# Layer 0 of a four-layer kernel: the preparation of each chunk spread over 24 slots, a column-ordered projection read contiguously and written permuted, and Z's copy placed ahead of the exponential

## The chip, the cores and the metric

The kernel runs on one core of one Trainium2 chip. The metric is the device time of one execution in microseconds, as the median of three runs. Engines are called as in the profile: PE is the matrix engine, PEld its weight loads, DVE the vector engine, ACT the scalar engine, POOL the general engine, SP the engine that issues DMA transfers here. A "q" behind a name (SPq) is the engine's sequencer.

## The reference

The model has four layers; only layer 0 is touched. After a group norm, an input projection and a depthwise convolution, it runs a selective scan in four directions (row order, column order, and both reversed) over 4096 positions, for 256 channels with 16 states each, for two batch elements:

```
dts, Bs, Cs = split(einsum('bkdl,kcd->bkcl', xs, x_proj_w))
dts   = einsum('bkrl,kdr->bkdl', dts, dt_proj_w)
delta = softplus(dts + dt_bias)
for each position:
    h = exp(delta * A) * h + (delta * u) * B
    y = sum over states of h * C
```

The four results are added in image order, normalised, gated and projected.

## The kernel before

**Tiling.** Each batch element is one pass of the same code. Its work is 32 chunks: four directions, in the order 0, 2, 1, 3, by eight chunks of 512 positions. Directions 1 and 3 read the image in column order. A chunk has two halves of 256 positions, and a half has eight slots; a slot holds four groups of 128 channel-state pairs by 256 positions. The list `todo` holds the chunks, `NS` is 512 slots, and the loop `for s in range(NS)` (from L471) is one slot per pass. `where(s)` turns a slot into chunk, direction, half and place `j` in the half. In this text slots of a chunk are counted 0 to 15, and the first half is 0 to 7.

**One slot.** All order is written by hand (`tc.manual_schedule`): each engine runs its instructions in the order in which the Python code issues them. A slot issues, in this order:

- `make_inputs(s + 2)` in even slots: on POOL, L391 multiplies a 1 MB tile `row` (delta times u, one row for eight channels, repeated over the states by the load) by `bt` (B) into the state tile `S`, for two slots. L396 and L397 add the carried state. `S` has two buffers, each for one half of a chunk.
- `decays(s + 2)`: four PE products at L411 give delta times A in one of three PSUM tiles `dA`.
- `exponent(s + 1)`: ACT takes exp of `dA` at L425.
- the scan on DVE at L482, in place in `S`.
- one step of `contract` (L432 on), a generator that sums the states of the previous half. Its products (L443) write one PSUM tile `Z`, four times per half; ACT copies `Z` to `ze` (L449), and SP stores it (L453). It has seven steps, in places 0 to 6 of a half, and products in steps 0 to 5. The tile `W` (C, from L430) is loaded in places 2 to 5, for use in the next half.
- one step of each open `prologue`, the generator that prepares a chunk.
- `load_rows(s + 7)` in odd slots: the next `row` (L379), with three buffers.

**The preparation.** `prologue(i + 2)` starts in slot 1 of chunk i and takes one step per slot, so parts of two prologues are open at a time. It projects u (L296, the product named px; `in_order` gives u in the order of the direction), copies the result to `xd` (L299, L301), stores B and C to DRAM (`bcd`, L303 and L304), forms delta's argument (L311), computes softplus in pieces on ACT (L313 to L322) and POOL (L323, L325), sums the pieces on PE by a product with the identity (L333), copies delta to `dt` (L336), multiplies by u on DVE (L337), stores that to DRAM as `drow` (L339), and at the end gets `bt` (L346), `dg` (L344) and the factor `ea` for the carried state (L353, L354). The tiles `r`, `e`, `u`, `l` and `xd` have one buffer each. PSUM is full: three `dA` tiles of two banks, one bank for `Z` and one (tag `ps`) for all products of the prologue.

**SP.** Nearly all transfers of the layer are issued by SP in program order on one queue. The build gives them eight completion semaphores in turn, so a transfer is issued only once the one eight before it has landed.

Of the kernel before, what the change touches and what calls it, by code (L numbers as in the profile page):

```python
# [16 lines left out]
F32 = mybir.dt.float32  # L17
# [3 lines left out]
ALU = mybir.AluOpType  # L21
# [142 lines left out]
def layer0(k, x, x0):  # L164
# [14 lines left out]
    with ExitStack() as es:  # L179
# [21 lines left out]
        def in_order(h, kk, c):  # L201
            if kk % 2:
                u = U[:, h, :].rearrange("p (g i w j) -> p w g j i", g=4, i=16, w=4)[:, c // 2]
            else:
                u = U[:, h, (c // 2) * 1024 : (c // 2 + 1) * 1024].rearrange("p (i w j) -> p w i j", i=16, w=4)
            return u[:, 2 * (c % 2) : 2 * (c % 2) + 2]

        for b in range(B):
# [60 lines left out]
            with ExitStack() as e2:  # L269
# [19 lines left out]
                def prologue(i):  # L289


                    kk, c = todo[i]
                    m = 64 * (kk % 2)
                    px = ps.tile([P, CH], F32, name="pd", tag="ps")
                    for h in range(2):
                        nc.tensor.matmul(px[m : m + 64], w_xp[:, h, kk, :], in_order(h, kk, c), start=h == 0, stop=h == 1)  # L296
                    yield
                    xd = one.tile([P, CH], F32, name="xd")
                    nc.scalar.copy(xd[m : m + 32], px[m : m + 32])  # L299

                    nc.scalar.copy(xd[m + 32 : m + 64].rearrange("p (e t a r) -> p e t a r", e=4, t=4, a=8), px[m + 32 : m + 64].rearrange("p (e a t r) -> p e t a r", e=4, a=8, t=4))  # L301
                    bcd = ddr.tile([32, CH], F32, name="bcd")
                    nc.sync.dma_start(out=bcd[:16], in_=xd[m + 8 : m + 24, :])  # L303
                    nc.sync.dma_start(out=bcd[16:], in_=xd[m + 32 : m + 48, :])  # L304
                    yield
                    yield
                    r, e, u, l = (one.tile([P, 2, CH], F32, name=n) for n in ("r", "e", "u", "l"))
                    for h in range(2):
                        bias = k.v("dt_b")[:, kk * 2 + h : kk * 2 + h + 1]
                        pd = ps.tile([P, CH], F32, name="pd", tag="ps")  # L310
                        nc.tensor.matmul(pd, w_dt[m : m + 8, kk // 2, h * P : (h + 1) * P], xd[m : m + 8, :], start=True, stop=True)  # L311
                        yield
                        nc.scalar.activation(e[:, h, :], pd, AF.Abs, bias=bias)  # L313
                        nc.scalar.activation(r[:, h, :], pd, AF.Relu, bias=bias)
                        yield
                    nc.scalar.activation(e, e, AF.Exp, scale=-1.0)
                    yield
                    nc.scalar.activation(u, e, AF.Identity, bias=1.0)
                    yield
                    nc.scalar.activation(l, u, AF.Ln)  # L320
                    yield
                    nc.scalar.activation(u, u, AF.Identity, bias=-1.0)  # L322
                    nc.gpsimd.tensor_tensor(r, r, l, ALU.add)  # L323
                    yield
                    nc.gpsimd.tensor_tensor(e, e, u, ALU.subtract)  # L325
                    yield
                    yield
                    dt = two.tile([P, 2, CH], F32, name="dt")
                    drow = ddr.tile([2, 8, 8, 2, 2, T], F32, name="drow")
                    for h in range(2):  # L330
                        pd = ps.tile([P, CH], F32, name="pd", tag="ps")
                        for n, t in enumerate((r, e)):
                            nc.tensor.matmul(pd, k.ident, t[:, h, :], start=n == 0, stop=n == 1)  # L333
                        yield
                        v = lambda t: t.rearrange("p (a b c) -> p a b c", a=2, b=16)
                        nc.scalar.copy(dt[:, h, :], pd)  # L336
                        nc.vector.tensor_tensor(v(r[:, h, :]), v(pd), in_order(h, kk, c), ALU.mult)  # L337
                        for a in range(2):
                            nc.sync.dma_start(out=drow[:, :, :, a, h].rearrange("s d g t -> (d g) s t"), in_=r[64 * a : 64 * a + 64, h, :].rearrange("p (s t) -> p s t", s=2))  # L339
                        if h == 0:  # L340
                            yield
                    f = T - 1 if kk >= 2 else 0
                    dg = one.tile([P, 2, 16, 2], F32, name="dg")
                    nc.gpsimd.tensor_tensor(dg, pick.unsqueeze(1).unsqueeze(3).to_broadcast([P, 2, 16, 2]), dt[:, :, f::T].rearrange("p h s -> p s h").unsqueeze(2).to_broadcast([P, 2, 16, 2]), ALU.mult)  # L344
                    bt = two.tile([P, CH], F32, name="bt")
                    nc.sync.dma_start(out=bt, in_=bass.AP(bcd.tensor, bcd.offset, [[CH, 16], [0, 8], [1, CH]]))  # L346
                    for _ in range(7):
                        yield
                    pe = ps.tile([P, CH], F32, name="pd", tag="ps")
                    nc.tensor.matmul(pe[:, :64], own, dg.rearrange("p s g h -> p (s g h)"), start=True, stop=True)  # L350
                    yield
                    ea = two.tile([P, 2, 32], F32, name="ea")
                    nc.vector.tensor_tensor(ea, pe[:, :64].rearrange("p (s g) -> p s g", s=2), an2[:, kk * 32 : kk * 32 + 32].unsqueeze(1).to_broadcast([P, 2, 32]), ALU.mult)  # L353
                    nc.scalar.activation(ea, ea, AF.Exp)  # L354
                    ready[i] = dt, drow, bcd, bt, ea


                NS = 16 * len(todo)
# [73 lines left out]
                def contract(n):  # L432

                    i, kk, sub, _ = where(8 * n)
                    S, W = Ss[n], Ws[n % 2]
                    t0 = (todo[i][1] * CH + sub * T) // P
                    for f in range(4):
                        Z = pz_.tile([P, 4, 32, 4], F32, name="Z")
                        for a in range(4):
                            for q in range(4):  # L440
                                w = W[:, f // 2].rearrange("p d t -> p (d t)")[:, 16 * (f % 2) + 4 * a + q :: 32]
                                t = 64 * f + 16 * a + q
                                nc.tensor.matmul(Z[32 * q : 32 * q + 32, :, :, a].rearrange("p t g -> p g t"), w, S[:, :, t : t + 13 : 4], start=True, stop=True)  # L443
                            if a == 1 and f in (0, 3):
                                yield
                        yield
                        if f % 2 == 0:
                            ze = two.tile([P, 4, 32, 8], F32, name="ze")
                        nc.scalar.copy(ze[:, :, :, 4 * (f % 2) : 4 * (f % 2) + 4], Z)  # L449
                        if f % 2:  # L450
                            for t in range(4):
                                dst = ydr[b][kk, t0 + f // 2, 4 * t : 4 * t + 4].rearrange("q d g a -> (q d) (g a)")
                                nc.sync.dma_start(out=dst, in_=ze[t::4, t].rearrange("p g a -> p (g a)"))  # L453

                with tc.manual_schedule():
# [10 lines left out]
                    decays(1)  # L466
                    exponent(0)
                    soon, back = [prologue(1)], None
                    for _ in range(15):
                        next(soon[0])  # L470
                    for s in range(NS):  # L471
                        i, kk, sub, j = where(s)
                        S, dA = Ss[s // 8], dAs[s % 3]
                        if j % 2 == 0:
                            make_inputs(s + 2)
                        if s % 16 == 1 and i + 2 < len(todo):
                            soon.append(prologue(i + 2))
                        decays(s + 2)
                        exponent(s + 1)
                        s_ = slice(None, None, -1) if kk >= 2 else slice(None)  # L480
                        flat, dflat = (t.rearrange("p g t -> p (g t)")[:, s_] for t in (S[:, 4 * j : 4 * j + 4, :], dA))
                        nc.vector.tensor_tensor_scan(flat, dflat, flat, 0.0, ALU.mult, ALU.add)  # L482
                        if j == 0 and s > 0:
                            back = contract(s // 8 - 1)
                        if back is not None:
                            if next(back, back) is back:
                                back = None
                                del Ss[s // 8 - 1]
                        if j in (2, 3, 4, 5):
                            for d in (2 * j - 4, 2 * j - 3):  # L490
                                load_c(s // 8, d)
# [1274 lines left out]
```

## Time and profile before

| What | us |
|---|---|
| Median of three runs | 15351.72 |
| Lowest and highest | 15348.02, 15357.47 |
| The profiled execution's own time | 15384.23 |
| Its span | 15382.4 |
| First scan to last scan of the first batch element | 177.7 to 1815.5 |
| First scan to last scan of the second | 2198.4 to 3843.7 |

The profile page and all times inside it are of one execution, whose span is 15382.4 us; some 3283 us of it (1637.8 + 1645.3) are the two loops that the change touches. Within a row of groups, the first numbers behind the bar are busy time and mean ns of one instruction, then idle time of the engine just before, with the instruction that ended it. Matmul ends are modelled and overlap, so the time of a stream of products is read from start to start. A product in f32 stands as two records.

### The profile page before, as it was taken

How to read it: one execution, taken by the hardware profiler on the slowest of the kernel's cores; microseconds unless marked ns; L12 is line 12 of the kernel's file. 1: busy time of each engine (PE TensorE's matmuls, PEld its weight loads, DVE VectorE, ACT ScalarE, POOL GpSimd, SP SyncE). 2: the span in 40 equal slices, each digit the busy share in tenths (PEclk: the TensorE clock that was granted, in tenths of full speed). 3: DMA queues.
4: the chain of work that ended last, by engine and by line, in shares of the span. 5: the costliest groups of instructions: out<-in, count | busy, mean ns of one | idle time of the engine just before them, and what ended most of it. 6: DMA issues, size and time to landing. Idle time of an engine off the chain costs nothing.

```text
span 15382.4 us, 234681 instructions
## 1 busy us (share of the span) xinstructions
PE 12387.6 (81%) x91214; PEld 7926.4 (52%) x91214; DVE 12707.2 (83%) x11405; ACT 9497.0 (62%) x14103; POOL 13019.5 (85%) x4168
## 2 busy tenths in 40 slices
PE   7888788888777545497896888978888899898897
PEld 4544454444577413254563555645445555555565
DVE  6777657777453799999999999999999999999973
ACT  4666436655001477777777677777777777777752
POOL 5888638888287899999999999999999999999960
PEclk8999899999888767698997999989999999999998
DMA  6888748888565445465555555555666666666543
GB/s 158 200 194 196 187 105 197 197 195 191 166 199 162 148 151 167 155 203 180 194 193 171 185 189 193 199 185 191 200 190 201 191 196 204 191 196 200 189 161 134
DMA packets 1444903, 2809.37 MB, mean 183 GB/s; under 512 B 393136, under 2 KB 1110608, under 8 KB 1240784
## 3 DMA queue, kind: packets, MB, share of 16 engines
q1 hardware_dynamic: 1395936, 2638.55, 58.3%
q0 software_dynamic: 46560, 153.18, 3.3%
q8 instruction: 721, 11.81, 0.3%
q14 instruction: 390, 3.19, 0.1%
q10 hardware_dynamic: 1296, 2.63, 0.0%
HBM read 2372.53 MB, written 421.31 MB: 182 GB/s over the span
## 4 chain that ended last, share of the span: by engine, by line
POOL 43%; PE 23%; DVE 12%; DMA 10%; issue 4%; ACT 3%; SPq 3%; another core or an unknown queue 1%; POOLq 0%; ACTq 0%; DVEq 0%
POOL S L1318 36%; DVE S L1376 9%; PE pef L1202 6%; DMA row<-drow 6%; POOL S L391 3%; PE Z L443 3%; PE Z L1336 2%; POOL G L742 2%; PE dA L411 2%; DMA W<-bcd 2%; PE acc L1175 2%; SPq L430 1%; DVE S L482 1%; PE pv L756 1%; PE pd L333 1%
## 5 line engine op out<-in xcount | busy, mean ns | idle before, releaser
L1376 DVE TENSOR_TENSOR_SCAN S<-dA,S 128x512 f32<-128x512 f32 x8192 | 9225.7, 1199 | 387.5 <-ACT dA L1374 204.1
L1318 POOL TENSOR_TENSOR S<-row,g 128x4096 f32<-128x4096 f32 x1024 | 9104.3, 8898 | 241.4 <-DMA row<-drow 159.7
L1374 ACT ACTIVATE dA<-row,a_t 128x512 f32<-128x512 f32 x8192 | 5614.6, 692 | 2165.9 <-DVE S L1376 2131.1
L1336 PE MATMUL Z<-S,cv 128*32 128x256 f32 x32768 | 2506.4, 436 | 1508.1 <-ACT ze L1342 1230.9
L1202 PE MATMUL pef<-hk,ur 128*128 128x256 f32 x14336 | 3514.1, 388 | 134.7 <-ACT e L1182 116.7
L1202 PEld LDWEIGHTS pef<-hk,ur 128*128 128x128 f32 x14336 | 2646.9, 191 | 1074.4 <-issue 564.1
L482 DVE TENSOR_TENSOR_SCAN S<-dA,S 128x1024 f32<-128x1024 f32 x1024 | 2309.3, 2283 | 758.6 <-ACT dA L425 422.8
L391 POOL TENSOR_TENSOR S<-row,bt 128x2048 f32<-128x2048 f32 x512 | 2383.8, 4656 | 432.8 <-PE Z L443 334.3
L1336 PEld LDWEIGHTS Z<-S,cv 128*32 128x32 f32 x32768 | 1003.4, 121 | 2718.1 <-issue 1229.5
L443 PE MATMUL Z<-S,W 128*32 128x128 f32 x16384 | 1191.5, 434 | 438.4 <-DMA W<-bcd 218.1
L1342 ACT COPY ze<-Z 128x512 f32<-128x512 f32 x1024 | 1122.4, 1096 | 232.5 <-PE Z L1336 196.2
L425 ACT ACTIVATE dA<-dA 128x1020 f32<-128x1020 f32 x1024 | 1028.6, 1010 | 378.0 <-PE dA L411 339.3
L411 PE MATMUL dA<-dt,quad 64*128 64x255 f32 x8192 | 1183.4, 414 | 19.8 <-DVE S L482 19.3
L443 PEld LDWEIGHTS Z<-S,W 128*32 128x32 f32 x16384 | 715.0, 170 | 818.3 <-issue 288.1
L1175 PE MATMUL acc<-e,mw 128*128 128x512 f32 x1920 | 1048.4, 634 | 29.6 <-ACT e L1182 28.8
L411 PEld LDWEIGHTS dA<-dt,quad 64*128 64x128 f32 x8192 | 750.9, 195 | 580.4 <-issue 385.3
L1202 PEld LDWEIGHTS pef<-hd,ur 128*128 128x128 f32 x4096 | 758.3, 194 | 493.7 <-issue 235.0
L742 POOL DMA_INDIRECT G<-table,idx x576 | 807.2, 1401 | 219.8 <-issue 167.9
L1202 PE MATMUL pef<-hd,ur 128*128 128x256 f32 (+1 forms) x4096 | 876.7, 340 | 102.0 <-ACT e L1182 95.5
L749 DVE TENSOR_TENSOR G<-G,wt 128x4608 f32<-128x4608 f32 x64 | 317.8, 4966 | 557.0 <-DMA G<-table,idx 537.2
L1182 ACT COPY e<-pef 128x512 f32<-128x512 f32 x960 | 557.9, 587 | 109.6 <-PE pef L1202 60.7
L756 PE MATMUL pv<-ident,G 128*128 128x128 f32 x4608 | 569.2, 285 | 30.0 <-issue 29.6
(341 smaller groups left out, 7858.9 us busy)
## 6 DMA issues: line engine op xcount, KB each, us to landing
row<-drow SPq DMA_DIRECT2D x1536, 1024.0 KB
zd<-ze SPq DMA_DIRECT2D x1024, 256.0 KB
hk<-in_phi_dram SPq DMA_DIRECT2D x128, 576.5 KB
hk<-in_phi_dram SPq DMA_DIRECT2D x96, 704.5 KB
hd<-in_phi_dram SPq DMA_DIRECT2D x512, 128.5 KB
mw<-wdr SPq DMA_DIRECT2D x480, 128.0 KB
hk<-in_phi_dram SPq DMA_DIRECT2D x160, 320.5 KB
hk<-in_phi_dram SPq DMA_DIRECT2D x96, 448.5 KB
```

What stands on the lines that cost most here:

```text
L391: nc.gpsimd.tensor_tensor(S[:, o, :], rows.pop(s), bt[:, sub * T : (sub + 1) * T].unsqueeze(1).to_broadcast([P, 8, T]), ALU.mult)
L411: nc.tensor.matmul(dA[:, 2 * a + h, rest], stats[d, j][r, h, :], dt[r, h, at : at + T - 1], start=True, stop=True)
L443: nc.tensor.matmul(Z[32 * q : 32 * q + 32, :, :, a].rearrange("p t g -> p g t"), w, S[:, :, t : t + 13 : 4], start=True, stop=True)
L482: nc.vector.tensor_tensor_scan(flat, dflat, flat, 0.0, ALU.mult, ALU.add)
L742: nc.gpsimd.indirect_dma_start(out=G[:, o, :], out_offset=None, in_=table[b], in_offset=bass.IndirectOffsetOnAxis(ap=idxs[b][:, i * 9 + o ...
L1175: nc.tensor.matmul(acc.rearrange("p a s -> p (a s)"), ms[f][:, o, :], e, start=box["first"], stop="whole" in box and (f, o) == todo[-1])
L1202: nc.tensor.matmul(pe[:, a, 256 - n :], ur[:, par, j, :], h[:, at : at + n], start=i == 0, stop=i + 1 == len(mm))
L1318: nc.gpsimd.tensor_tensor(S, row.unsqueeze(1).to_broadcast([P, 2, R, T]), g.unsqueeze(2).to_broadcast([P, 2, R, T]), ALU.mult)
L1336: nc.tensor.matmul(Z[32 * j : 32 * j + 32, q], cv[:, h, s], S[:, h, :, s], start=h == 0, stop=h == 1)
L1342: nc.scalar.copy(ze.rearrange("p q t e -> p q e t"), Z)
L1374: nc.scalar.activation(dA, row[:, j % R, :], AF.Exp, scale=a_t[:, h, d : d + 1])
L1376: nc.vector.tensor_tensor_scan(s, dA, s, 0.0, ALU.mult, ALU.add)
```

## The change

The prologue starts in slot 5 instead of 1, is stepped ahead of the older one (`insert(0, ...)`), and its steps are spread out. For chunk i + 2, counted from slot 0 of chunk i (16 is slot 0 of chunk i + 1):

| Step | slot before | slot after |
|---|---|---|
| px, the projection of u | 1 | 5 |
| copies to xd, stores of bcd | 2 | 6 |
| delta's argument, halves of the channels | 4 and 6 | 8 and 10 |
| Abs and Relu | 5 and 7 | 9 and 11 |
| exp, +1, Ln | 8, 9, 10 | 12, 13, 14 |
| -1 (ACT) and r + l (POOL) | 11 | 15 |
| e - u (POOL) | 12 | 17 |
| sum of the pieces on PE | 14 and 16 | 22, both |
| copy to dt, product with u, four drow stores | 15 and 17 | 23, all |
| dg and the load of bt | 17 | 24 |
| product for ea; ea | 24; 25 | 28; 29 |

The second sum of the pieces now has a PSUM tile of its own, `pd1`, in `Z`'s bank. The order of the row loads does not change: the first `row` of chunk i + 2 is issued in slot 25 in both. Before the loop, 11 instead of 15 steps of the second chunk's prologue are run.

In directions 1 and 3 px reads u with contiguous runs of 16 and writes PSUM with a step of 16 elements (64 bytes); before, it read with a step of 64 elements and wrote contiguously.

The step of `contract`, with the copy of `Z`, is issued between the decays and the exponential of a slot; before, after the scan.

```diff
-                    m = 64 * (kk % 2)
+                    m, box = 64 * (kk % 2), [None] * 5
+                    ready[i] = box
...
                     for h in range(2):
-                        nc.tensor.matmul(px[m : m + 64], w_xp[:, h, kk, :], in_order(h, kk, c), start=h == 0, stop=h == 1)
+                        to, u = px[m : m + 64].rearrange("p (a b c) -> p a b c", a=2, b=16), in_order(h, kk, c)
+                        if kk % 2:
+                            to, u = (t.rearrange("p a b c -> p a c b") for t in (to, u))
+                        nc.tensor.matmul(to, w_xp[:, h, kk, :], u, start=h == 0, stop=h == 1)
...
                     nc.gpsimd.tensor_tensor(r, r, l, ALU.add)
                     yield
+                    yield
                     nc.gpsimd.tensor_tensor(e, e, u, ALU.subtract)
-                    yield
+                    for _ in range(5):
+                        yield
+                    pds = [ps.tile([P, CH], F32, name="pd", tag="ps"), pz_.tile([P, CH], F32, name="pd1", tag="Z")]
+                    for h in range(2):
+                        for n, t in enumerate((r, e)):
+                            nc.tensor.matmul(pds[h], k.ident, t[:, h, :], start=n == 0, stop=n == 1)
                     yield
...
                     for h in range(2):
-                        pd = ps.tile([P, CH], F32, name="pd", tag="ps")
-                        for n, t in enumerate((r, e)):
-                            nc.tensor.matmul(pd, k.ident, t[:, h, :], start=n == 0, stop=n == 1)
-                        yield
-                        v = lambda t: t.rearrange("p (a b c) -> p a b c", a=2, b=16)
-                        nc.scalar.copy(dt[:, h, :], pd)
-                        nc.vector.tensor_tensor(v(r[:, h, :]), v(pd), in_order(h, kk, c), ALU.mult)
+                        nc.scalar.copy(dt[:, h, :], pds[h])
+                    for h in range(2):
+                        nc.vector.tensor_tensor(v(r[:, h, :]), v(pds[h]), in_order(h, kk, c), ALU.mult)
                         for a in range(2):
                             nc.sync.dma_start(out=drow[:, :, :, a, h].rearrange("s d g t -> (d g) s t"), in_=r[64 * a : 64 * a + 64, h, :].rearrange("p (s t) -> p s t", s=2))
-                        if h == 0:
-                            yield
+                    box[:3] = dt, drow, bcd
+                    yield
...
-                    for _ in range(7):
+                    box[3] = bt
+                    for _ in range(4):
                         yield
...
-                    ready[i] = dt, drow, bcd, bt, ea
+                    box[4] = ea
...
-                        Z = pz_.tile([P, 4, 32, 4], F32, name="Z")
+                        Z = pz_.tile([P, 4, 32, 4], F32, name="Z", tag="Z")
...
-                    for _ in range(15):
+                    for _ in range(11):
                         next(soon[0])
...
-                        if s % 16 == 1 and i + 2 < len(todo):
-                            soon.append(prologue(i + 2))
+                        if s % 16 == 5 and i + 2 < len(todo):
+                            soon.insert(0, prologue(i + 2))
                         decays(s + 2)
-                        exponent(s + 1)
-                        s_ = slice(None, None, -1) if kk >= 2 else slice(None)
-                        flat, dflat = (t.rearrange("p g t -> p (g t)")[:, s_] for t in (S[:, 4 * j : 4 * j + 4, :], dA))
-                        nc.vector.tensor_tensor_scan(flat, dflat, flat, 0.0, ALU.mult, ALU.add)
                         if j == 0 and s > 0:
                             back = contract(s // 8 - 1)
                         if back is not None:
                             if next(back, back) is back:
                                 back = None
                                 del Ss[s // 8 - 1]
+                        exponent(s + 1)
+                        s_ = slice(None, None, -1) if kk >= 2 else slice(None)
+                        flat, dflat = (t.rearrange("p g t -> p (g t)")[:, s_] for t in (S[:, 4 * j : 4 * j + 4, :], dA))
+                        nc.vector.tensor_tensor_scan(flat, dflat, flat, 0.0, ALU.mult, ALU.add)
```

More of the change, by code (lines that the diff above doesn't have):

```diff
@@ L329, in prologue @@
                     drow = ddr.tile([2, 8, 8, 2, 2, T], F32, name="drow")
+                    v = lambda t: t.rearrange("p (a b c) -> p a b c", a=2, b=16)
                     for h in range(2):
-                        pd = ps.tile([P, CH], F32, name="pd", tag="ps")
-                        for n, t in enumerate((r, e)):
-                            nc.tensor.matmul(pd, k.ident, t[:, h, :], start=n == 0, stop=n == 1)
-                        yield
-                        v = lambda t: t.rearrange("p (a b c) -> p a b c", a=2, b=16)
-                        nc.scalar.copy(dt[:, h, :], pd)
-                        nc.vector.tensor_tensor(v(r[:, h, :]), v(pd), in_order(h, kk, c), ALU.mult)
+                        nc.scalar.copy(dt[:, h, :], pds[h])
+                    for h in range(2):
+                        nc.vector.tensor_tensor(v(r[:, h, :]), v(pds[h]), in_order(h, kk, c), ALU.mult)
                         for a in range(2):
                             nc.sync.dma_start(out=drow[:, :, :, a, h].rearrange("s d g t -> (d g) s t"), in_=r[64 * a : 64 * a + 64, h, :].rearrange("p (s t) -> p s t", s=2))
-                        if h == 0:
-                            yield
+                    box[:3] = dt, drow, bcd
+                    yield
                     f = T - 1 if kk >= 2 else 0
```

## The prediction

> **What bounds the kernel now.** I read the groups of the page first, for the size of what can move.
>
> ```profile
> L482 DVE TENSOR_TENSOR_SCAN S<-dA,S 128x1024 f32<-128x1024 f32 x1024 | 2309.3, 2283 | 758.6 <-ACT dA L425 422.8
> L391 POOL TENSOR_TENSOR S<-row,bt 128x2048 f32<-128x2048 f32 x512 | 2383.8, 4656 | 432.8 <-PE Z L443 334.3
> L443 PE MATMUL Z<-S,W 128*32 128x128 f32 x16384 | 1191.5, 434 | 438.4 <-DMA W<-bcd 218.1
> ```
>
> The scans are busy 2309 us of the two loops' 3283 and idle 759, so the scan's duration does not set the pace. POOL idles 334 us because the buffer of S that it wants is still read by Z's products. Next I took stages in the steady part:
>
> ```profile
> core 0: us, PE busy (x) PEld busy (x) DVE busy (x) ACT busy (x) POOL busy (x), PEclk, DMA share, GB/s
> 500.00:1000.00 500.00, 424.19 (x3836) 247.27 (x3836) 363.11 (x189) 307.69 (x373) 428.47 (x215) 0.95 0.86 198
> 1000.00:1500.00 500.00, 436.42 (x3869) 245.98 (x3872) 366.97 (x186) 306.82 (x376) 420.48 (x210) 0.97 0.85 196
> ```
>
> POOL, PE and the DMA engines are each at about 85%: no single one is the bound; each waits for another in turn. From the scan's start times, a chunk of chunks 1 to 29 takes 51.9 us: 26.6 in slots 0 to 7, 25.3 in slots 8 to 15. At 85%, POOL needs 44 us a chunk (8 x 4.66 at L391, 8 x 0.21 and 2 x 0.23 at L397 and L396, 2.34 + 2.41 + 0.32 of the preparation: 44.5), the DMA engines 44.4 (0.855 x 51.9). DVE needs 38 (16 x 2.26, 2 x 0.93). So 45 us is the floor of any reordering, and some 7 us a chunk are loss. Where that loss sits is seen in the order of time, slot 6 of one chunk and px of two others:
>
> ```profile
> 703.75 4.52 POOL L391 TENSOR_TENSOR S<-row,bt 128x2048 f32<-128x2048 f32 x1 [4.69 <-PE Z L443]
> ...
> 741.04 1.93 PE L296 MATMUL pd<-U,w_xp 128*64 128x512 f32 x4
> ...
> 1313.47 3.64 PE L296 MATMUL pd<-U,w_xp 128*64 128x512 f32 x4
> ```
>
> The POOL wait comes in one place: averaged over chunks, 5.1 us before the L391 of slot 6, at most 0.2 elsewhere. In slots 0 to 5 the products of Z share PE with one L333 (2.0), px (1.9 in row order, 3.6 in column order) and two L311 (1.1 each): 6 to 8 us in front of the last Z that frees S. DVE pays in slot 8 (2.6 us for POOL). In slots 9 to 12 it pays for late C and for Ln:
>
> ```profile
> PE Z L443 <- DMA W<-bcd: 218.1, 87, 5.5
> ACT ea L354 <- DVE ea L353: 226.0, 63, 5.9
> ```
>
> There ACT stands 3.6 us for ea, then runs Ln with two table loads (1.28 each) between two exponentials; the scan of slot 12 waits 2.5 us on average.
>
> **Slots 0 to 7 after.** Take the start of scan 0 as 0 and PE's own durations: four products of dA take 1.06 from start to start, a step of Z 1.2 or 2.2 (steps 3 and 4). Products of dA may start when the scan three slots back is done. dA(2) is done at 0; slots 0 and 1 bring Z to 4.5, slot 2 to 7.8, slot 3 to 11.1, slot 4 to 13.3, slot 5 has Z's end at 15.6. POOL by then has done two L391 and e - u (4.9 + 2.4 + 5.1), and ends the third at 17; it finds S free. The 5.1 us wait goes. px follows to 17.7 and dA(8) to 18.8, then both L333: 3.9 us, to 22.7. ACT copies the second half to dt until 23.4 and DVE multiplies until 24.2. Scan 7 was over at about 19, so DVE has a new wait of some 4 us there, with scan 8 queued behind it: the stall moves from POOL to DVE, and shrinks. Slots 0 to 7: 24.2 instead of 26.6, gain 2.4.
>
> **Slots 8 to 15 after.** W for these slots is loaded with no drow or bt in front of it on SP's queue (they now leave in slots 7 and 8), so Z starts unhindered; its own new wait, for pd1 in its bank, ends with the second product with u, when PE is still at dA (0 added; without that cover, up to 1 us). PE has Z 8.9, dA 8.5, L311 2.2, L350 0.7: 20.3 against 18.1 of scans. Going through slot by slot as above, PE sets scans 13 to 15 back by 2 us, and Ln with its loads, now in slots 14 and 15, holds exp(16) back 2.3 us: 1.0 + 2.43 + 1.28 + 1.0 on ACT between the ends of exp(15) and exp(16), 4.7 in all, against 2.3 of the scan between. That gives 22.2. The order of POOL's adds changes nothing in its sum.
>
> **The wait that is added there.** r has one buffer. The Relu of the next prologue (slot 9, before: four slots after drow's last store, now two) must wait until drow has landed. Let R be the end of the second product with u. SP issues two stores of 0.6 us each; from issue to the last semaphore increment, drow took 4.9 us in the median (2.4 to 5.8 between the 5th and 95th of 100). It lands at R + 6.2. Behind the Relu on ACT stand the copy of Z and exp(11), 0.7 + 0.6 + 1.0; scan 11 wants exp(11) at R + 6.8. So the Relu must start by R + 4.5: a stall of 1.7 us, with ends 0 (2.4 us of latency) and 5.6 (8.8, the median of a 1 MB row on the same queue). I take 1.7, drow's own row. Slots 8 to 15: 23.9 instead of 25.3, gain 1.4.
>
> The same landing holds SP: the row of slot 9 is the first that reads the new drow. Behind it stand two loads of W, four stores of ydr and the next row. It would be issued at R + 7 and goes at R + 6.2 to 7: with 9 us to land, POOL has it at R + 16, and wants it in slot 14, at about R + 17. Costed at 0; if the landing is late by more than 1 us, it costs the rest.
>
> **px permuted.** The trace has no product that reads contiguously and writes with a 64-byte step. The Trainium skill's page SBUF — State Buffer, section "Door 1: The DMA port swizzle", says PSUM has lines of two f32 and that any write pattern that is not contiguous slows products much. That speaks against the change: px would stay at 3.6 us or worse. The nearest row is layer 0's last stage:
>
> ```profile
> 1917.03 1.16 PE L538 MATMUL py<-ident,y 128*64 128x128 f32 x8
> ```
>
> L538 writes with a step of two elements, a new line for each. (1160 - 277) / 7 / 128 is 0.99 ns a column; px in row order, contiguous on both sides, has (1930 - 592) / 3 / 512 = 0.87, px in column order (3640 - 1037) / 3 / 512 = 1.69. By the row the permuted px takes 0.59 + 3 x 512 x 0.99 = 2.1 us; by the rule 3.6. The upper end is from Z (L443), which writes and reads with steps at 16 records in 1.24: if its four column groups ran fully side by side, 1.7 to 2.4 ns a column, 4.9 us. I take 2.1, and have used it: the column-ordered chunks lose nothing against 1.9. By the rule, 29 chunks lose 1.5 us, and the sum is 44 us worse.
>
> **Z's copy ahead of the exponential** adds 0.59 in front of exp(s + 1) in four of eight slots, and may wait there for Z's products of the slot before; exp(s + 1) has the running scan of 2.26 as cover. Z's next products waited 158 us in all for that copy; the part of it in slots 2 to 5 is already in the times above, where PE never waits for ACT. Without the cover it would cost 0.6 x 8, 5 us a chunk.
>
> **Sum.** 24.2 + 23.9 = 48.1 a chunk, against 51.9; 3.8 x 58 chunks = 220. Chunks 0, 30 and 31 have parts of the preparation alone (46, 47.5 and 43 us), and I leave them. Before the first scan POOL's e - u falls behind the second L391; scan 0 may start 8 us sooner, but POOL's row of work ends at the same time: 0. 15384 - 220 = 15164 for the profiled execution, whose own time of 15384 is 33 above the median of the runs; 15132 on their scale.
>
> **Rivals.** First, the wait takes another place, and about half the gain goes: px slow, 44 us; POOL short of rows, as DMA would have to run at 0.92 of its time (44.4 / 48.1) where SP stops for stores; POOL already waits 1.5 us a chunk for rows. With 1.3 us a chunk more, 75: 15132 + 44 + 75 = about 15250. For it: three resources within 2 us of each other. Against: the queue idles 7 to 8% of the time now, in slots 5, 6 and 13.
>
> Second, slower, by drow's landing alone. If drow lands as late as the rows it follows, each us of latency over 4.9 comes out of every chunk: at 8.7 us the gain is gone, at 10 a chunk takes 53.2 and the kernel 15352 + 58 x 1.3 = 15427. For it: rows themselves take 7 to 10. Against: the row before it was issued in slot 5, 9 us earlier, and 4.9 was measured with rows in the queue.
>
> Third, no change: DMA is the true bound and eats what is freed. But chunk 30, with all of its rows and the first half's C, ran in 47.5, so the queue can do that pace.
>
> Fourth, better: no stall for drow and none at Ln, 46 us a chunk, 15010.
>
> **How the numbers follow.** Mine 0.61, half the gain 0.20, slower 0.10, no change 0.05, better 0.04. What a measurement of this kernel can tell from no change is about 0.2%, 31 us. Faster: 0.61 + 0.20 + 0.04 = 0.85; same 0.05; slower 0.10. My own case alone runs from 15060 (46.9 a chunk) to 15205. The range for 8 in 10 takes the half case in: 15040 to 15290.
>
> **What would show it.** POOL's wait for Z at L391 falls from 334 us to under 60. DVE waits before the product with u grow from 162 to some 250. Relu at slot 9 (L318 in the new kernel) shows a wait for drow of some 2 us a chunk; scan 12's wait of 2.5 us goes, and scan 16's rises. px in column order stands at about 2.1 us. POOL's and the DMA's busy shares rise to 0.92. I am wrong if Relu stands 5 us or more for drow, if rows keep POOL waiting over 3 us a chunk, or if px takes over 3.6 us.

## The result and the profile after

The changed kernel takes 15399.58 us (median of 18 runs, 15369.36 to 15422.54). The kernel before, run on the same chips, takes 15375.15 us (18 runs, 15344.09 to 15384.19). The ratio is 1.0019, with a 95% interval of 1.0012 to 1.0026. The forecast was 15132 us, in a range of 15040 to 15290, on the scale of the three runs then known (15351.72): the gain of 220 us did not come, and some 25 us were lost.

The profiled execution took 15392.59 us (span 15390.8), 8 us over that of before. The two loops took 1669.4 and 1661.9 us, 3331 together, against 3283: 48 us more. Of these, 24 came back ahead of the loops, where fewer steps of the second chunk's preparation stand (the first scan starts at 165.8 instead of 177.7, and the second loop 371 instead of 383 us after the first), and 16 behind the two loops, in what the change doesn't touch. A chunk of chunks 1 to 29 takes about 52.3 us (26.9 in slots 0 to 7, 25.5 in slots 8 to 15), against 51.9 (26.5 and 25.4 by the same reading) and a forecast of 48.1. These chunks are 26 of the 48 us; the other 22 are in chunks 0, 30 and 31, which the sum left out. Chunk 0 alone, which starts sooner now, takes 52.1 and 52.6 us in the two loops instead of 46.5 and 45.6.

The groups of the changed kernel's page, in the same columns as before (busy time, mean ns, idle time just before, what ended most of it):

```profile
L496 DVE TENSOR_TENSOR_SCAN S<-dA,S 128x1024 f32<-128x1024 f32 x1024 | 2304.4, 2281 | 816.7 <-ACT dA L433 452.6
L399 POOL TENSOR_TENSOR S<-row,bt 128x2048 f32<-128x2048 f32 x512 | 2375.6, 4641 | 494.9 <-DMA row<-drow 333.0
...
L451 PE MATMUL Z<-S,W 128*32 128x128 f32 x16384 | 1192.3, 434 | 306.7 <-DMA W<-bcd 172.3
```

The durations are those of before. What changed is the releaser of POOL: it waited 334 us for Z, and now waits 333 us for rows. Its idle time as a whole grew from 433 to 495 us, that of the scans from 759 to 817. The stages in the steady part of the changed kernel, in the columns shown before (busy time and count of each engine, then clock, DMA share and GB/s):

```profile
500.00:1000.00 500.00, 421.88 (x3830) 243.66 (x3826) 356.30 (x186) 297.15 (x373) 416.59 (x213) 0.94 0.87 194
1000.00:1500.00 500.00, 421.77 (x3812) 243.86 (x3814) 360.76 (x184) 295.91 (x369) 421.12 (x208) 0.93 0.88 194
```

The forecast wanted POOL and DMA at 0.92. POOL is at 0.83 and 0.84 (416.59 and 421.12 of 500), DMA at 0.87 and 0.88. The granted clock is 0.94 and 0.93, against 0.95 and 0.97 before, and a record of dA's products takes 423 ns in the mean instead of 414. That is not what separates the kernels: the run with all of the change but the inner spreading, below, has 0.92 and 429 ns and is faster than the kernel before. The waits of the two loops (from 170 to 3880 us), as what waited, for what, total, times and longest:

```profile
DVE S L496 <- ACT dA L433: 452.6, 277, 4.1
...
POOL S L399 <- DMA row<-drow: 322.1, 117, 10.5
...
PE Z L451 <- DMA W<-bcd: 172.3, 53, 7.2
ACT r L318 <- DMA drow<-r: 153.4, 54, 5.3
DVE r L344 <- ACT dt L342: 149.1, 120, 22.5
...
POOL S L399 <- PE Z L451: 123.3, 56, 5.1
```

By slot, averaged over all chunks: before the multiply of slot 6, POOL waits 0.14 us for Z (before the change 5.07). In slot 12 it now waits 4.1 us for a row, and in slot 14 another 2.5, most of it for Z (1.8). So 5 us a chunk were gained in one place and 6.5 lost in two others. One chunk in order of time shows how, with lines from the timeline of each engine, SP's first, then DVE's, ACT's, DVE's and POOL's, of the changed kernel (start, duration; idle time before and its releaser in brackets). It begins at 582; slot 7 begins at about 605.

```profile
606.79 4.44 SPq L461 DMA_DIRECT2D ydr<-ze  x4
...
612.41 4.63 SPq L346 DMA_DIRECT2D drow<-r  x4
617.14 1.24 SPq L387 DMA_DIRECT2D row<-drow  x1
...
610.59 0.69 DVE L344 TENSOR_TENSOR r<-pd,U 128x512 f32<-128x512 f32 x1 [1.02 <-ACT dt L342]
...
619.62 0.69 ACT L318 ACTIVATE r<-pd,pv 128x512 f32<-128x512 f32 x1 [4.46 <-DMA drow<-r]
...
621.73 2.29 DVE L496 TENSOR_TENSOR_SCAN S<-dA,S 128x1024 f32<-128x1024 f32 x1 [3.89 <-ACT dA L433]
...
620.18 0.21 POOL L405 TENSOR_TENSOR S<-S,st 128x8 f32<-128x8 f32 x1
624.74 4.82 POOL L399 TENSOR_TENSOR S<-row,bt 128x2048 f32<-128x2048 f32 x1 [4.36 <-DMA row<-drow]
...
633.11 4.53 POOL L399 TENSOR_TENSOR S<-row,bt 128x2048 f32<-128x2048 f32 x1 [3.26 <-PE Z L451]
```

The second product with u ends at 611.28. All four stores of `drow` now stand together on SP's queue, and the `row` of slot 7 (for slots 14 and 15 of the running chunk) stands behind them. That row doesn't read the `drow` being stored; it reads the one of the running chunk and could have left as soon as its buffer was free, at 607.8, when the multiply of slot 6 ended. It leaves at 617.14, and POOL, free at 620.39, gets it at 624.7. On the other side, the Relu at 619.62 waits until the stores have landed, because they read `r` and `r` has one buffer. The copy of Z and an exponential stand behind it on ACT, so a scan starts 3.9 us late, and POOL's next buffer comes free 3.3 us late. One event, the packed stores, has two followers: a row, and the Relu.

### The profile page after: what moved, and what is told of

Its sections match the earlier page's. It is cut to its first block, busy times and chain, and to the rows that moved or that the text cites. A ratio compares the mean times of both kernels' runs of the same rounds, so it can differ in the third digit from the quotient of the medians.

```text
span 15390.8 us, 234714 instructions
## 1 busy us (share of the span) xinstructions
PE 12357.3 (80%) x91214; PEld 7921.5 (51%) x91214; DVE 12690.9 (82%) x11405; ACT 9445.0 (61%) x14103; POOL 13014.7 (85%) x4168
## 4 chain that ended last, share of the span: by engine, by line
POOL 44%; PE 21%; DVE 13%; DMA 12%; issue 5%; ACT 2%; SPq 2%; POOLq 0%; DVEq 0%; ACTq 0%
POOL S L1326 34%; DVE S L1384 11%; DMA row<-drow 8%; PE pef L1210 6%; POOL S L399 5%; POOL G L750 3%; PE Z L1344 2%; PE Z L451 2%; PE acc L1183 2%; PE dA L419 1%; DVE S L496 1%; PE pw L926 1%; POOL r L327 1%; PE pd L336 1%; SPq L438 1%
## 5 line engine op out<-in xcount | busy, mean ns | idle before, releaser
L399 POOL TENSOR_TENSOR S<-row,bt 128x2048 f32<-128x2048 f32 x512 | 2375.6, 4641 | 494.9 <-DMA row<-drow 333.0
L419 PE MATMUL dA<-dt,quad 64*128 64x255 f32 x8192 | 1226.2, 423 | 215.0 <-DVE S L496 214.2
L1350 ACT COPY ze<-Z 128x512 f32<-128x512 f32 x1024 | 1123.2, 1097 | 237.2 <-PE Z L1344 201.6
L457 ACT COPY ze<-Z 128x512 f32<-128x512 f32 x512 | 299.2, 584 | 910.7 <-PE Z L451 888.4
```

Source lines behind the costliest of these rows:

```text
L399: nc.gpsimd.tensor_tensor(S[:, o, :], rows.pop(s), bt[:, sub * T : (sub + 1) * T].unsqueeze(1).to_broadcast([P, 8, T]), ALU.mult)
L419: nc.tensor.matmul(dA[:, 2 * a + h, rest], stats[d, j][r, h, :], dt[r, h, at : at + T - 1], start=True, stop=True)
L1350: nc.scalar.copy(ze.rearrange("p q t e -> p q e t"), Z)
```

## The experiments

All kernels compute the full result. Ratios are to the kernel before, with 95% intervals.

### One of the two waits at a time

First `r` alone gets two buffers, so that the Relu needn't wait for the stores.

```diff
-                    r, e, u, l = (one.tile([P, 2, CH], F32, name=n) for n in ("r", "e", "u", "l"))
+                    r, e, u, l = ((two if n == "r" else one).tile([P, 2, CH], F32, name=n) for n in ("r", "e", "u", "l"))
```

> The changed kernel with r in two buffers and nothing else, so that the Relu of the next preparation no longer waits for drow to land (153 us of ACT's waits in the changed kernel, 2.4 a chunk). Theory 1, late transfers: drow's landing and the rows issued behind it take back what POOL's wait for Z gave. Then the waits of the scans in slots 11 to 13 (4.5 us a chunk) fall to under 2.5, POOL's wait for Z in slot 14 (1.8) goes, POOL's wait for the row of slot 7 (4.1 us a chunk, at L399 of slot 12) stays, and the time falls by about 2 us a chunk, to some 15280. Rival A, packing: both sums on PE in slot 6 and DVE standing in slot 7 set the pace: no change, 15380 to 15410. Rival B, the DMA engines are the true bound at 85% busy: the wait for rows grows by what the Relu gives up, 15370 to 15410.

Measured: 15404.43 us, ratio 1.0016 (1.0006 to 1.0025), as the changed kernel. The waits of its loops:

```profile
POOL S L399 <- DMA row<-drow: 436.0, 214, 10.8
...
POOL S L399 <- PE Z L451: 10.6, 10, 1.9
```

The Relu's wait is gone and POOL's for Z with it (123 to 11 us). But the wait for rows grew from 322 to 436: POOL comes to the late row sooner, and stands for it longer.

Next, one more buffer for rows beside that, with the order on SP left as it is.

```diff
-                rp = e2.enter_context(tc.tile_pool(name=f"l0r{b}", bufs=3))
+                rp = e2.enter_context(tc.tile_pool(name=f"l0r{b}", bufs=4))
```

> As before, and row with four buffers instead of three, at the same places in the order of issue. A row then no longer waits for the L399 just before it, but in the order of SP it still stands behind drow's stores. Theory 1: POOL's wait for rows falls from 5 us a chunk to under 2, a chunk takes 48 to 49 us, and the kernel 15150 to 15210. Rival A, packing: 15370 or more. Rival B, DMA as the bound: the wait for rows moves to other slots and the time is 15330 or more, with the DMA share still under 0.88.

Measured: 15404.08 us, 1.0014 (1.0004 to 1.0023), POOL's wait for rows 443 us. A buffer doesn't help a load that stands behind stores: it is the order of issue, not the space, that makes the row late.

The other half alone: the row load is issued ahead of the prologue's step in its slot, with one buffer of `r` and three of `row`.

```diff
-                        soon = [g for g in soon if next(g, g) is not g]
                         if j % 2 == 1 and i + 1 < len(todo) or s + 7 < NS and j % 2 == 1:
                             load_rows(s + 7)
+                        soon = [g for g in soon if next(g, g) is not g]
```

> The changed kernel with the next row's load ahead of the preparation's step and nothing else (r one buffer, row three). If r's single buffer costs nothing here either, as e1 seemed to show: 15310 to 15340, as e5. If it mattered in e5, since drow now lands one row later (4.7 us at the queue's pace of 220 GB/s) and the Relu waits for it: 15380 or more.

Measured: 15437.81 us, 1.0033 (1.0022 to 1.0045), slower than the changed kernel. The waits of its loops:

```profile
POOL S L399 <- PE Z L451: 492.1, 74, 10.9
...
ACT r L318 <- DMA drow<-r: 210.5, 58, 7.2
...
POOL S L399 <- DMA row<-drow: 32.6, 20, 10.8
```

The rows are in time (322 to 33 us). The Relu stands longer, since the stores leave after the row, and POOL pays for it: the wait for Z in slot 14 is 7.6 us a chunk.

### Both together

`r` from the pool of two, four buffers for rows, and the row ahead of the prologue's step.

> The changed kernel with r in two buffers, row in four, and the load of the next row issued ahead of the preparation's step, so that in slot 7 it stands in front of drow's four stores and no longer behind them. Theory 2, the place on SP: POOL's 4.2 us a chunk before the L399 of slot 12 are there because SP stands at drow's stores until DVE has multiplied, while POOL has run ahead; that wait falls under 1.5 us. Part of it comes back in slot 14, whose row must wait for drow to land. All of POOL's waits for rows and loads go from 7.6 to some 4 us a chunk, and the time from 15404 to 15230 to 15300. Rival B, the DMA engines as the bound: the waits move and their sum stays above 7, 15380 or more.

Measured: 15320.17 us, 0.9968 (0.9958 to 0.9977), with 51.2 us a chunk. The waits of its loops:

```profile
POOL S L399 <- DMA row<-drow: 215.3, 132, 10.6
...
POOL S L399 <- PE Z L451: 147.5, 36, 7.2
```

The row of slot 12 is waited for 0.4 us instead of 4.1, and the Relu doesn't stand. Taken alone, neither edit gains; together, with the fourth row buffer, they take some 80 us off the changed kernel. That shows that the two waits are parallel: while one stands, removing the other gains nothing. It doesn't settle all: POOL now stands 4.3 us in slot 14 (2.2 for Z, 1.3 for a row, 0.7 for W). Slots 8 to 15 take 23.7 us now, but slots 0 to 7 still take 27.5. Whether the fourth row buffer is needed here was not separated.

Rows issued a whole pair of slots earlier, with `r` and the row buffers as above, but behind the prologue's step (one more row, `load_rows(8)`, is loaded before the loop):

```diff
                         if j % 2 == 1:
-                            load_rows(s + 7)
+                            load_rows(s + 9)
```

> The changed kernel with r in two buffers, row in four, and every row loaded two slots earlier (in the odd slot s the row for s + 9). The row of the old slot 7 is issued in slot 5, well ahead of drow; the first row that reads the new drow is issued in slot 7, straight behind its stores, and holds SP until they have landed. Theory 2: POOL's wait at the L399 of slot 12 goes, at slot 14 some 2 us stay, time 15200 to 15280. Rival B: 15380 or more.

Measured: 15523.49 us, 1.0101 (1.0084 to 1.0118), the slowest of all. The waits of its loops up to 3900 us (they end at 3993):

```profile
POOL S L399 <- PE Z L451: 492.4, 106, 7.6
PE Z L451 <- DMA W<-bcd: 458.2, 59, 14.5
...
POOL S L399 <- DMA bt<-bcd: 67.5, 11, 8.4
...
POOL S L399 <- DMA row<-drow: 26.8, 13, 11.6
```

Rows hardly keep POOL waiting now, but `bt` and `W` are late: Z's products wait 458 us for W instead of 172. The first row that reads the new `drow` is issued in slot 7, right behind the stores, and SP stands there until they have landed, 120 us in both loops. That can't be all of it, since SP stands 209 us for `drow` in the faster run before this one. SP also stands 508 us at the loads of W until an earlier row has landed, against 355 in that run. Which of the two makes W late was not separated.

### The parts of the change alone

The permuted projection alone, in the kernel before:

```diff
-                        nc.tensor.matmul(px[m : m + 64], w_xp[:, h, kk, :], in_order(h, kk, c), start=h == 0, stop=h == 1)
+                        to, u = px[m : m + 64].rearrange("p (a b c) -> p a b c", a=2, b=16), in_order(h, kk, c)
+                        if kk % 2:
+                            to, u = (t.rearrange("p a b c -> p a c b") for t in (to, u))
+                        nc.tensor.matmul(to, w_xp[:, h, kk, :], u, start=h == 0, stop=h == 1)
```

> The kernel before with the permuted px alone, which takes 1.9 us instead of 3.6 in the 32 column-ordered chunks. In the kernel before, px stands in slot 1 ahead of Z's products that free S, where POOL waits 5 us: theory 1 has POOL's wait for Z shrink by what px gives up in those chunks, 1.7 x 30, and the time about 15325. Rival B, DMA as the bound: no change, 15360 to 15390.

Measured: 15361.84 us, 0.9984 (0.9975 to 0.9994). In the column-ordered chunks, slots 0 to 7 fell from 27.3 to 26.0 us, and POOL's mean wait for Z in slot 6, over all chunks, from 5.1 to 4.3. It is a gain, a small one.

The step of `contract` put back behind the scan, in the changed kernel:

> The changed kernel with the step of contract, and so Z's copy, put back behind the scan. All else as in the changed kernel. Theory 1 has the copy's place matter little, because ACT's waits for Z do not stand in front of a late exponential in most slots: 15370 to 15430. Rival C, the copy's new place is what cost the gain (865 us of ACT's waits are now for Z, ahead of an exponential): the time falls to 15300 or less.

Measured: 15418.38 us, 1.0025 (1.0015 to 1.0034). The interval overlaps that of the changed kernel, so the two can't be told apart here. POOL waits 275 us for rows and 185 for Z, where the changed kernel has 322 and 123: the sum is about the same. In the kernel before, with the permuted projection, the same move has more in it:

> The kernel before with the permuted px and with Z's copy ahead of the exponential, without the spreading. Both were worth something alone or taken out (24 us for px in the kernel before, 14 for the copy in the changed one). If they add: 15330 to 15350. If the copy helps only where the preparation is spread: 15355 to 15370. Rival C, the copy's place costs: 15375 or more.

Measured: 15312.43 us, 0.9962 (0.9948 to 0.9976). Against the projection alone, the copy takes another 0.2% off; the two intervals just touch.

The later place alone: before, with the prologue started in slot 5 instead of 1, and nothing spread inside it. The entry in `ready` is filled in before `bt` and `ea` exist, and 11 instead of 15 steps stand before the loop.

```diff
-                        if s % 16 == 1 and i + 2 < len(todo):
+                        if s % 16 == 5 and i + 2 < len(todo):
                             soon.append(prologue(i + 2))
```

> The kernel before with the preparation started in slot 5 instead of 1 and nothing else: each step keeps its distance from the others, both sums of the pieces stay in two slots (2 and 4), px falls in slot 5, delta's argument in 8 and 10, drow's stores in slots 3 and 5. Theory 2: the gain of the changed kernel's new phase without its packed stores; POOL's wait for Z (5.1 us in slot 6) falls to about 3, as 4 us of products stand ahead of Z's last instead of 5 to 7, and the rows behind drow are early enough: 15290 to 15350. Rival B: 15365 to 15400.

Measured: 15318.48 us, 0.9965 (0.9953 to 0.9976), 51.0 us a chunk. POOL's wait for Z in slot 6 falls to 1.3 us; rows keep it waiting 187 us in all, against 322 in the changed kernel. Here the stores of `drow` stay in two pairs, two slots apart.

All of the change but the spreading of the steps inside the prologue (with `pd1` and the order of the two open prologues, which belong to it), that is, this place, the projection and the copy together:

> The kernel before with the start of the preparation in slot 5, the permuted px and Z's copy ahead of the exponential: all of the change but the spreading inside the preparation (its sums stay in two slots, 2 and 4, with drow's stores in slots 3 and 5, and no second PSUM tile). Against the changed kernel it is that spreading alone. Theory 2: the parts are worth 0.35% (phase) and 0.38% (px and copy), and overlap, as both shorten POOL's wait for Z; 0.5 to 0.7% faster than before, 15265 to 15295, so that the spreading inside costs some 110 us. Rival B, a shared floor near 51 us a chunk from the DMA engines: no better than each part, 15310 to 15330.

Measured: 15315.87 us, 0.9953 (0.9939 to 0.9967), 51.0 us a chunk. This is the whole change with one part left out, and it is faster than before, where the change is slower. 1.0019 by 0.9953 is 1.0066: the inner spreading as it is built costs 0.7%, some 100 us. The waits of its loops (L395 is the multiply that is L399 in the changed kernel):

```profile
POOL S L395 <- DMA row<-drow: 197.5, 139, 10.9
...
POOL S L395 <- PE Z L447: 102.9, 93, 1.7
```

The parts don't add up. The projection and the copy gave 0.4% and the place 0.35%, together 0.5%. The three intervals overlap, so it isn't shown that both together are better than one. With the row load ahead of the step as well (and four row buffers):

> As the one before it, with row in four buffers and the next row's load ahead of the preparation's step. Drow's stores stand in slots 3 and 5 here, in front of rows that POOL wants in slots 8 and 10, where it waits 1.5 and 0.7 us. Theory 2: these two waits go, 1 to 2 us a chunk, 15190 to 15250 if the one before it is at 15280. Rival B: no change against it.

Measured: 15324.44 us, 0.9964 (0.9950 to 0.9977), no better. The wait for rows went from slot 10 to slot 12, and its total stayed (200 us). With the stores in two pairs the move gains nothing.

### Another place for the packed stores

The changed kernel with its whole preparation eight slots earlier (19 steps of `prologue(1)` and 3 of `prologue(2)` before the loop), alone:

```diff
-                        if s % 16 == 5 and i + 2 < len(todo):
-                            soon.insert(0, prologue(i + 2))
+                        if s % 16 == 13 and i + 3 < len(todo):
+                            soon.insert(0, prologue(i + 3))
```

> The changed kernel with the whole preparation eight slots earlier and nothing else: r has one buffer, row three, and the row of slot 15 stands behind drow's stores. If the place of the stores just before the first row that reads them is the cause of the loss: 15285 to 15325, near e11. If the buffers and the order of the row made e11's gain, and the place did not: 15380 to 15410, as the changed kernel.

Measured: 15415.94 us, 1.0016 (1.0007 to 1.0026). The waits of its loops:

```profile
POOL S L399 <- DMA row<-drow: 332.2, 126, 10.8
...
ACT r L318 <- DMA drow<-r: 135.5, 51, 4.8
...
POOL S L399 <- PE Z L451: 127.2, 59, 4.4
```

The three sums of the changed kernel (322, 153, 123) come again, and the row is waited for in slot 4 instead of 12. The place alone is not what costs, then: the packed stores cost the same there, by what stands behind them. And with both waits taken away as above:

> The changed kernel with r in two buffers, row in four and the row ahead of the stores, as e5, and the whole preparation eight slots earlier: drow's stores in slot 15 instead of 7, ten slots ahead of the first row that reads them. All packing on PE and DVE stays, half a chunk off. If what is left of the loss after e5 is that the first row must wait for drow (POOL's 4.4 us in slot 14 with what hangs on it): 15230 to 15280. If it is the packing on PE and DVE and Ln between two exponentials (rival A): as e5, 15305 to 15340.

Measured: 15286.39 us, 0.9936 (0.9921 to 0.9951), 50.6 us a chunk, the fastest kernel here: faster than before by 0.64%, than the changed one by some 110 us. Its waits and its stages in the steady part:

```profile
POOL S L399 <- PE Z L451: 330.6, 63, 6.8
...
POOL S L399 <- DMA row<-drow: 43.7, 35, 11.0
```

```profile
500.00:1000.00 500.00, 438.96 (x3972) 252.30 (x3973) 367.73 (x193) 305.92 (x383) 435.74 (x218) 0.95 0.88 202
1000.00:1500.00 500.00, 437.63 (x3966) 252.10 (x3956) 375.87 (x192) 309.03 (x384) 438.77 (x223) 0.95 0.88 203
```

The rows are in time, and POOL waits for Z in slot 6, 5.1 us a chunk. That is not the old wait left over: with everything eight slots earlier, slot 6 stands to the preparation as slot 14 does in the changed kernel, and slot 14, which is the changed kernel's slot 6, has no wait (0.05). The halves have changed places too: slots 0 to 7 take 23.5 us, slots 8 to 15 take 27.1. POOL and PE are at 0.87 to 0.88. What is won here is won on rows and the Relu, and, against the same edits with the stores in slot 7 (0.9968), another 0.3% by the place, where the first row that reads the new `drow` no longer waits for it.

## Why the prediction was wrong

Two terms of the sum failed: a row that stands behind the stores was put at nothing, and POOL was taken as free at the start of slots 0 to 7. The runs show the price of the first, together with the Relu's wait. The second is nearly all of what is left, and its cause is in part open.

- **The wait for Z in slot 6 goes: right.** 5.07 us became 0.14. But it goes only there; see slots 0 to 7 below.
- **The new stand of DVE in slot 7: right in kind, smaller in size.** About 4 us were costed, and 250 us of L344's waits were forecast; they are 149 us, 22.5 of them ahead of the second loop, so some 2.0 a chunk, in the stretch shown 1.39 and 1.02. But scan 7 itself came later than costed.
- **The Relu's wait for `drow`: right, 2.4 us a chunk instead of 1.7.** Two errors stand against each other. Landing took 2.4 to 3.9 us in the median of each store, not 4.9. Issue was later: the working let SP issue the last two stores right after the products. In the stretch shown SP is busy with `ydr` and `bcd` until 612.3, and the four stores take until 617.04, 5.8 us behind the second product; 3.9 is the median. So the last store lands 6.1 us behind the product in the median, where 6.2 was costed: the sum of the two is right by luck.
- **"The same landing holds SP: the row of slot 9 ... Costed at 0": this is the step that failed.** It looked only at the row that reads the new `drow`. The row of slot 7 doesn't read it, stands behind the four stores all the same, and was not costed at all. It leaves 4.0 us behind the second product in the median (5.9 in the stretch shown) and lands 7.4 us later. POOL waits 4.1 us for it. Both halves of the price are seen in the runs: with the row moved ahead its wait goes (322 to 33 us), and the time falls only with the Relu's wait gone too. Taken away together (with the fourth row buffer) they are worth 80 us with the stores in slot 7, and 110 with the place changed as well, of the 268 us between forecast and result. So this step is not the whole miss.
- **The half slots 0 to 7 at 24.2: wrong, and only in part as a consequence.** 26.9 was measured. The working took POOL as free to run ahead: two multiplies and e - u by slot 5. POOL comes out of slots 12 and 14 some 6.5 us of waiting late, and the scans of slots 2 and 4 stand 1.7 and 2.9 us for it. Of the 6.5, 4.1 are the row above. The rest is in slot 14, where POOL wants the other buffer of `S`; most of it is for Z, which the Relu holds back (123 us to 11 with `r` in two buffers). The sum followed the release of `S` in slot 6 and nowhere else. With the row in time and the Relu free, slots 8 to 15 take 23.7 us (23.9 was forecast), but slots 0 to 7 take 27.5, and POOL still stands 4.3 us in slot 14. With the preparation eight slots earlier it stands 5.1 us for Z at that same point of it. There, as much stands at one change of buffer as had left the other. POOL is the chain: 44.5 us of work and some 7.5 of waits make the chunk of 52. Before the change the waits were 6.6, and in the fastest kernel they are 5.9. Why they hardly shrink stays open.
- **Ln in slots 14 and 15: right.** 2.3 us costed; scan 16 (slot 0) stands 2.29 us for its exponential. The terms as they are written add to 5.7, not 4.7: the first 1.0, exp(15) itself, lies ahead of the stretch. 4.7 is what the trace has in the median. And 18.1, 2 and 2.3 are 22.4, not 22.2.
- **px permuted: right, and better than costed.** 2.1 us was taken; 1.93 came.
- **Before the loops: costed at 0, nearly right.** The first scans start 24 us sooner in sum, but chunk 0 takes 12.6 us longer in sum, and chunks 30 and 31, which were left out, 9.5.
- **The floor of 45 us: not reached by any kernel.** The best has 50.6. POOL, PE and the DMA engines, which each need 44 to 45 us, with two buffers of S between them, lose some 6 us or more in every order tried here. A third buffer of S wasn't tried, so its share stays open. So does what the stand in slot 7 and Ln cost by themselves; no run takes one of them away alone.

The signs named beforehand did point to it: "if rows keep POOL waiting over 3 us a chunk" came true with 5.0. The rival of half the gain had the rows too, but as a shortage of DMA's pace. The DMA engines were at 0.87 to 0.88 in the changed kernel, and at 0.88 in the fastest one: what was short was the order of issue, not the pace. The rival of a loss by `drow`'s landing had the right event and the wrong follower: it put the price in landing, which was quicker than costed.

What remains inferred is why the late rows cost little before. The kernel before has stores ahead of rows too, in slots 15 and 1, and POOL waited little for rows:

```profile
POOL S L391 <- DMA row<-drow: 86.2, 89, 10.8
```

Most likely its wait for Z covered them. The run with `r` in two buffers speaks for it, since there too a wait taken away in one place came back at the row; no run shows it in the kernel before itself.

## What to carry to other kernels

When steps are packed or moved, list every instruction that stands behind them on each in-order queue, and not only those that read what they write: a prefetch that needs nothing of the store ahead of it is late all the same. Where one event holds two engines by two ways (here a row for POOL, a buffer for ACT), each removal alone can show nothing or a loss, as here, where only both together showed the gain. When a wait for a double-buffered tile goes at one change of buffer, follow the waiting engine to the other one before the gain is counted. A wait on the bounding engine is not gained until the next thing that it needs is in time as well.

## What the runs showed of the hardware

A product that writes PSUM with a 64-byte step ran at the pace of a contiguous one. The column-ordered projection in the changed kernel, from the timeline of PE:

```profile
1336.46 1.93 PE L300 MATMUL pd<-U,w_xp 128*64 128x512 f32 x4
```

That is the row-ordered projection's 1.93 us to the digit; read with a step and written contiguously, it was 3.64. The rule of the Trainium skill that was weighed in the prediction (SBUF — State Buffer, "Door 1: The DMA port swizzle") is not borne out by this f32 product, as far as it speaks of the write: the strided write into PSUM cost nothing, and it was the strided read that was dear.

The stores of `drow` landed sooner in the changed kernel: 4.9 us in the median before, 2.4 to 3.9 after, while the rows took 8.8 us in both. It is not that they are issued together: in the run with both waits taken away they are packed too, and took 5.3. What goes with it is a row under way. Stores issued while the last row had not landed took 4.9 us in the median before, 5.0 in the run with all but the inner spreading, 5.3 with both waits taken away, and 4.0 in the changed kernel; those issued with no row under way took 2.5 in the changed kernel and in the run with all but the inner spreading.
